# Exponentials of scores and router logits as pieces of their own in the interleaved attention block of a cross-attention and mixture-of-experts kernel

## The chip, the cores and the metric

The kernel runs on one core of a Trainium2 chip. A time is the device time of one execution in microseconds (us). Five engines work side by side, each in the order of its own instruction stream: TensorE (PE in the profile; its weight loads are PEld), VectorE (DVE), ScalarE (ACT), GpSimd (POOL) and SyncE (SP, which here only issues DMAs). They wait for one another through semaphores. An instruction that waits holds up everything behind it on its engine.

## The reference, cut to what matters

The input x has 4 batches of 512 rows of 256 numbers, the context 4 batches of 1024 rows.

```python
x = x + xattn(layernorm(x), ctx, mask)      # 16 heads of 16, 1024 keys, softmax, w_o
h = layernorm(x)                            # from here on the 4 batches attend to each other:
ln1 = layernorm(h)*w1 + b1; q, k, v = split(ln1 @ qkv.T)
p = softmax(q_s,b . k_t,b over earlier positions t)   # axes are (S, B): x's batches are "positions"
h2 = h + attn @ proj.T; ln2 = layernorm(h2)*w2 + b2
gate = softmax(ln2 @ router.T); top 2 of 8 experts
moe = sum over the 2 chosen of gate_e * (gelu(ln2 @ w1[e]) @ w2[e])
x = x + h2 + moe
```

The second block reads its first axis as the sequence, so a row of batch b attends to the same row of batches 0 to b: at most four scores for each head. That is the inner attention block of this case. It needs the rows of batch b after the big cross attention of that batch, and the keys and values of earlier batches.

## The kernel before, in words

**The big attention is the clock of the first stage.** It is cut into 16 groups m (batch m // 4, four heads each), each into 8 steps; a step is called T, from -10 to 128. In a step (loop at the end of the `with ExitStack()` block) PE computes four score tiles of 128x512 for the maxima of the group 10 steps ahead (`maximum`, L1116), which DVE reduces straight from PSUM (L1123, 512 times); four tiles of scores of the group itself (`numerators`, L1137), which ACT turns into exponentials (L1145, 512 times); and four products of the previous step's exponentials with the values (`products`, L1155). From T = 118 on there are no maxima left, so a step is shorter.

**Everything else is woven into these steps by a planner** (class `Plan`). A piece of work has a first and a last step, a cost on PE (`cost`), a cost on DVE (`vector`) and pieces that it must follow by a number of steps (`lag`). `spread` gives each piece a step, by due time, cost per step and a limit on DVE's; `level` then moves pieces to even out the estimated lengths of the steps. Within a step the pieces come after the step's own work, in order of their due times. So when a piece is put into a step, all its instructions on all engines are queued there.

**The inner attention, second layer norm and router of one half of a batch (256 rows) are a generator, `half(b, h)`.** Each `next` runs it to its next `yield`. For b of 0 to 2 the planner's table `PARTS` has one entry for each such part: (PE cost, lag, DVE cost). With their lines, the parts that matter: q, k and v (L438 to L448); the products of queries and keys on POOL (L479); the sums that make scores, their maximum and the subtraction on DVE (L490 to L492), and in the same part their exponential on ACT (L495, 128x64 to 128x128 numbers); normalising (L497 to L499); the products with the values on POOL (L504) and their sum (L515 for the last batch, L522); transposing and projecting (L290, L532, L539); statistics, and the rows written to the output by POOL's addition and an SP DMA (L545 to L548); router logits on PE (L568), their maximum and subtraction on DVE (L579, L580), and in the same part their exponential on ACT (L583); the choice of two experts (L585 to L607); positions in the experts' lists (L615 to L636); four indirect DMAs by POOL that put the rows into a table in DRAM (L659). Batch 0 has no scores to compute, so its generator only yields there.

**Not all of batch 2 is planned into the steps.** `parts[: -1 - 5 * h]` leaves the last part of half (2, 0) and the last six of half (2, 1) to the second stage. Batch 3 (`last`) is done there entirely, and there its exponentials already stand behind a `yield` of their own.

**The second stage** starts when the big attention ends. 39 tiles of 128 rows, each of one expert, are taken from the table (lists a, b, c, d of 9, 8, 9 and 13 tiles, loaded by SP at L800). A tile is transposed (`psxe` L1383, ACT L1386), multiplied by w1 (`psu` L1398), put through gelu on ACT (L1407), transposed (`psg` L1412, ACT L1414), multiplied by w2 (`psy` L1420), scaled on ACT (L1431) and added to the output by an indirect DMA that POOL issues (L1432). Between the tiles' pieces `others` puts the parts of the remaining halves, in an order written down ahead by a small model of the engines' times: the strings at the yields ("D3!" and the like) are its costs.

The generator's parts of batch 2 and the table meet in these lines, which the change touches:

```python
parts = PARTS[:-2] + PADS + PARTS[-2:] if b + h == 0 else PARTS
if b == 2:
    parts = parts[: -1 - 5 * h]
...
last = start + (28, 34, 0)[b] if b < 2 else END - 2 + h
chain = plan.chain(start, last, parts, behind=p, other=chain)
```

`chain` makes part n of the second half wait for part n + 3 of the half before it (`other`).

Of the kernel before, what the change touches and what calls it, by code (L numbers as in the profile page):

```python
# [55 lines left out]
class Plan:  # L56
# [19 lines left out]
    def chain(self, first, last, pieces, behind=None, other=()):  # L76


        slack = last - first - sum(p[1] for p in pieces)
        at = first  # L80
        chain = []
        for n, (cost, lag, vector, f, args) in enumerate(pieces):
            at += lag
            behind = self.add(
                cost,
                at,
                at + max(slack * (n + 1) // len(pieces), 0),
                f,
                *args,
                behind=behind,  # L90
                lag=lag,
                also=other[min(n + 3, len(other) - 1)] if other else None,
                vector=vector,
            )
            chain.append(behind)
        return chain
# [75 lines left out]
def kernel(  # L172
# [226 lines left out]
    def products_of(name, b):  # L399
        if b < B - 1:  # L400
            return k2.tile([P, B - 1, HALF, DK], F32, tag="pr", name=name, bufs=1)
        return late["pool"].tile([P, B, HALF, DK], F32, tag="prlast", name=name, bufs=2)

    def half(b, h):


        n = f"{b}_{h}"
        last = b == B - 1
# [26 lines left out]
        for i in range(2):  # L435
            ps = bank(f"psq{n}_{i}")
            for c in range(KC):
# [4 lines left out]
                    start=(c == 0),  # L442
# [9 lines left out]
        def of_batch(kv, j):  # L452

            return (
                kv[j][:, t0 : t0 + 2, :]
                .rearrange("p t (k d) -> p (t k) d", d=DK)
                .unsqueeze(2)
                .to_broadcast([P, 2 * KVH, REP, DK])
            )

        def grouped(x):
            return x.rearrange("p (k r) d -> p k r d", r=REP)

        if b == 0:

            yield
            yield
            yield
            at = k2.tile([P, HALF, DK], F32, tag="at", name=f"at{n}", bufs=1)
            nc.gpsimd.tensor_copy(grouped(at), of_batch(values, 0))  # L470
            yield
        else:

            def engine(j):
                return nc.vector if last and j % 2 else nc.gpsimd

            pr = products_of(f"pr{n}", b)
            for j in range(b + 1):
                engine(j).tensor_tensor(  # L479
                    grouped(pr[:, j]),  # L480
                    grouped(q.rearrange("p i (h d) -> p (i h) d", d=DK)),
                    of_batch(keys, j),
                    ALU.mult,
                )
            yield "D1.5|G2.4"
            sc = k2.tile([P, B, HALF], F32, tag="sc", name=f"sc{n}")[:, 0 : b + 1, :]
            top = k2.tile([P, HALF], F32, tag="top", name=f"top{n}")
            by_head = sc.rearrange("p j n -> p n j")
            over = [P, b + 1, HALF]
            nc.vector.tensor_reduce(sc, pr[:, 0 : b + 1], AX.X, ALU.add)  # L490
            nc.vector.tensor_reduce(top, by_head, AX.X, ALU.max)
            nc.vector.tensor_tensor(sc, sc, top.unsqueeze(1).to_broadcast(over), ALU.subtract)  # L492
            if last:
                yield "D3!"
            nc.scalar.activation(sc, sc, AF.Exp, scale=SCALE)  # L495
            yield "A2.9"
            nc.vector.tensor_reduce(top, by_head, AX.X, ALU.add)  # L497
            nc.vector.reciprocal(top, top)
            nc.vector.tensor_tensor(sc, sc, top.unsqueeze(1).to_broadcast(over), ALU.mult)  # L499
            yield "D1"  # L500
            at = k2.tile([P, HALF, DK], F32, tag="at", name=f"at{n}", bufs=1)
            pr = products_of(f"pv{n}", b)
            for j in range(b + 1):
                engine(j).tensor_tensor(  # L504
                    grouped(pr[:, j] if j or last else at),
                    of_batch(values, j),
                    sc[:, j, :]
                    .rearrange("p (k r) -> p k r", r=REP)
                    .unsqueeze(3)
                    .to_broadcast([P, 2 * KVH, REP, DK]),  # L510
                    ALU.mult,
                )
            if last:
                yield "D1.5|G2.4"
                nc.vector.tensor_reduce(  # L515
                    at.rearrange("p n d -> p (n d)"),
                    pr.rearrange("p j n d -> p (n d) j"),
                    AX.X,
                    ALU.add,
                )  # L520
            for j in range(1, 1 if last else b + 1):
                (nc.vector if b == 2 else nc.gpsimd).tensor_tensor(at, at, pr[:, j], ALU.add)  # L522
            yield "D2.2!"
# [5 lines left out]
        for i in range(2):  # L529
            ps = bank(f"psp{n}_{i}")  # L530
            for c in range(KC):
# [4 lines left out]
                    start=(c == 0),  # L536
# [29 lines left out]
        for i in range(2):  # L566
            for c in range(KC):
# [4 lines left out]
                    start=(c == 0),  # L572
# [5 lines left out]
        lgs = ps[:, 0 : 2 * E].rearrange("p (i e) -> p i e", e=E)  # L578
        nc.vector.tensor_reduce(m, lgs, AX.X, ALU.max)  # L579
        nc.vector.tensor_tensor(lg, lgs, m.to_broadcast(small), ALU.subtract)  # L580
        if last:
            yield "P1 D0.4!"
        nc.scalar.activation(lg, lg, AF.Exp)  # L583
        yield "A2.8"
        nc.vector.tensor_reduce(m, lg, AX.X, ALU.add)  # L585
# [85 lines left out]
    def pads(chosen, place):  # L671
# [19 lines left out]

    PARTS = [
        (0, 1, 1.7), (0, 2, 1.9), (0.45, 1, 0), (1.3, 1, 0.4), (1.3, 1, 0.4), (0, 1, 0), (0, 2, 1.8),
        (0, 1, 0.8), (0, 1, 0), (0.45, 2, 0), (0.86, 1, 0.5), (0.86, 1, 0.5), (0, 1, 1.4),
        (0, 2, 1.3), (0.45, 1, 0), (0.9, 1, 0.4), (0, 1, 1.7), (0, 1, 1.6), (1.1, 1, 1), (0, 1, 0),
        (0, 1, 0),
    ]
    PADS = [(0, 1, 0), (0, 2, 0), (0, 2, 0), (0, 2, 0)]
# [155 lines left out]
    def project_o(b, t):  # L854
# [10 lines left out]
        nc.vector.tensor_tensor(xt[:, b, t, :], ps[:, 0:D], xt[:, b, t, :], ALU.add)  # L865

    halves = {(b, h): half(b, h) for b in range(B) for h in range(2)}

    with ExitStack() as actx:
# [296 lines left out]
        def compact(dst, src):  # L1166
# [6 lines left out]
        plan = Plan()  # L1173
        START, END = -AHEAD, 8 * M + 1
        chain, queries = (), {}
        divided = [
            plan.add(
# [4 lines left out]
        for b in range(B):  # L1182
            first = 32 * b - 32
            if b:
                turned, projected = [], []
                for kc in range(NKC):
# [8 lines left out]
                        also=turned[kc - KRING] if kc >= KRING else None,  # L1195
# [17 lines left out]
                for h in range(2):  # L1213
# [10 lines left out]
                        also=x,  # L1224
# [10 lines left out]
            for kc in range(NKC):  # L1235
                start = 32 * b - 10 + kc if kc >= 4 else kc if b == 1 else 32 * b - 34 + kc
                start = max(start, START + 1)

                last = min(32 * b + kc - 2, 8 * M - 31)
# [15 lines left out]
            for h in range(2):  # L1255
                start = 32 * b + (40 if b < 2 else 38) + 4 * h
                parts = PARTS[:-2] + PADS + PARTS[-2:] if b + h == 0 else PARTS
                if b == 2:

                    parts = parts[: -1 - 5 * h]  # L1260
                parts = [(cost, lag, vector, next, (halves[b, h], None)) for cost, lag, vector in parts]
                last = start + (28, 34, 0)[b] if b < 2 else END - 2 + h
                chain = plan.chain(start, last, parts, behind=p, other=chain)
                p = None
            if b == 1:
# [74 lines left out]
        for T in range(START, END):  # L1340
            ahead[0] = T < 0
            n, kc = divmod(T, 8)
# [173 lines left out]
    n = 0  # L1516
# [106 lines left out]
```

## Time and profile before

| what | value |
|---|---|
| runs | 872.62, 872.97, 868.33 us; median 872.62 |
| the profiled execution's own time | 868.35 us |
| its span, first to last instruction | 866.6 us |
| first stage, up to the transposes of the last group (L837) | 642.2 us |
| second stage, from there on | 224.4 us |
| PE busy, ACT busy, DVE busy, POOL busy | 816.5, 476.8, 528.7, 311.3 us |
| mean granted PE clock | 0.985 |
| exponentials of the big attention (L1145) | 512, 596 ns each |
| maxima from PSUM (L1123) | 512, 684 ns each |
| exponentials of inner scores (L495), of router logits (L583) | 6 and 8, 282 and 215 ns each |
| additions to the output (L1432) | 39, 3.5 to 5.0 us from issue to landing |

How to read it: busy time is that of an engine's instructions; PE's are pipelined and their ends are modelled, so that PE busy 94% of the span is not PE at its peak. In the views of waits, "A <- B: 8.8, 4, 3.3" says that A sat idle for 8.8 us in total until B, 4 times, at most 3.3 us. In a timeline a row is start, length, engine, line, operation, and in brackets the idle time of the engine before it and what ended it.

### The profile page before, as it was taken

The page shows a single profiled execution, that of the slowest core. Times are in us where ns is not written, and L with a number is a line of the kernel's source. Part 1 is how long each engine was busy: PE and PEld are TensorE (multiplying, and loading weights), DVE is VectorE, ACT ScalarE, POOL GpSimd, SP SyncE. Part 2 cuts the span into 40 slices and gives each one's busy share as a digit, 9 for nine tenths or more (in the row PEclk, how much of TensorE's full clock was granted, in tenths as well). Part 3 has the DMA queues.
Part 4 walks back from the last instruction along what each step waited for, and adds up shares of the span by engine and source line. Part 5 has one row for each costly group of instructions (what it writes and reads, how often), then busy time and mean ns, then how long its engine had stood idle before and what let it go on. Part 6 is the DMA issues. An engine that isn't in the chain of part 4 may idle for free. (4 is left out here: it accounts for less than half of the span.)

```text
span 866.6 us, 14127 instructions
## 1 busy us (share of the span) xinstructions
PE 816.5 (94%) x5031; PEld 390.1 (45%) x5031; DVE 528.7 (61%) x1265; ACT 476.8 (55%) x959; POOL 311.3 (36%) x443
## 2 busy tenths in 40 slices
PE   5999999999999999999999999999989879999980
PEld 4543433334444334443433334333337557667650
DVE  6587666766677677887777778888455586100000
ACT  2326666656665655656656555555665647555430
POOL 7806251002363111579152201233224555433322
PEclk9999999999999999999999999999899999999996
DMA  7249003334000000001000009200212222552222
GB/s 228 57 133 301 17 1 118 110 99 128 2 1 1 25 14 13 34 17 51 1 1 1 13 2 334 99 20 2 69 38 55 53 36 58 121 98 27 29 31 24
DMA packets 46597, 53.30 MB, mean 62 GB/s; under 512 B 4782, under 2 KB 40580, under 8 KB 46528
## 3 DMA queue, kind: packets, MB, share of 16 engines
q1 hardware_dynamic: 37952, 41.42, 15.8%
q0 software_dynamic: 7920, 10.50, 6.9%
q8 instruction: 41, 0.67, 0.3%
q10 hardware_dynamic: 656, 0.48, 0.2%
q14 instruction: 28, 0.23, 0.1%
HBM read 22.43 MB, written 31.09 MB: 62 GB/s over the span
## 5 line engine op out<-in xcount | busy, mean ns | idle before, releaser
L1123 DVE TENSOR_REDUCE mx<-psm 128x1 f32<-128x512 f32 x512 | 326.6, 684 | 131.0 <-PE pss L1137 117.5
L1145 ACT ACTIVATE ex<-pss 128x512 f32<-128x512 f32 x512 | 277.5, 596 | 208.4 <-PE pss L1137 201.3
L1116 PE MATMUL psm<-kT_odd,shared 32*128 32x512 f32 x512 | 153.1, 639 | 1.1 <-DVE mx L1123 0.9
L1137 PE MATMUL pss<-qt,shared 32*128 32x512 f32 x512 | 152.7, 640 | 0.0
L1137 PE MATMUL pss<-qt,kT_odd 32*128 32x512 f32 x512 | 146.7, 649 | 0.5 <-ACT ex L1145 0.5
L1116 PE MATMUL psm<-shared 32*128 32x512 f32 x512 | 144.5, 639 | 2.2 <-ACT shared L1104 2.2
L1155 PE MATMUL av<-ex,vaug 128*32 128x512 f32 (+1 forms) x880 | 107.7, 559 | 0.0
L962 POOL TENSOR_TENSOR shared<-shared 128x256 f32<-128x256 f32 x44 | 33.3, 758 | 133.8 <-ACT shared L1005 101.7
L1420 PE MATMUL psy<-shared 128*128 x312 | 75.3, 383 | 4.6 <-ACT shared L1414 4.3
L1398 PE MATMUL psu<-shared 128*128 x156 | 76.0, 606 | 1.0 <-ACT shared L1431 0.4
L1116 PEld LDWEIGHTS psm<-kT_odd,shared 32*128 32x128 f32 x512 | 43.9, 183 | 72.5 <-DVE mx L1123 29.6
L1116 PEld LDWEIGHTS psm<-shared 32*128 32x128 f32 x512 | 43.3, 183 | 67.9 <-DVE mx L1123 25.7
L1420 PEld LDWEIGHTS psy<-shared 128*128 128x128 f32 x312 | 56.1, 190 | 13.4 <-ACT shared L1414 7.6
L1155 PEld LDWEIGHTS av<-ex,vaug 128*32 128x32 f32 x880 | 17.7, 108 | 84.3 <-issue 80.8
L659 POOL DMA_INDIRECT table<-rows,index x32 | 31.8, 994 | 53.8 <-issue 29.0
L264 POOL TENSOR_TENSOR rm<-vm,power 128x2 f32<-128x2 f32 x8 | 5.7, 712 | 117.6 <-DVE vm L545 114.7
L1137 PEld LDWEIGHTS pss<-qt,kT_odd 32*128 32x128 f32 x512 | 42.8, 186 | 8.3 <-issue 5.3
L1137 PEld LDWEIGHTS pss<-qt,shared 32*128 32x128 f32 x512 | 44.3, 183 | 0.6 <-ACT ex L1145 0.6
L964 POOL TENSOR_TENSOR shared<-shared 128x128 f32<-128x128 f32 x88 | 44.5, 527 | 0.0
L1407 ACT ACTIVATE shared<-psu 128x512 f32<-128x512 f32 x39 | 23.5, 603 | 26.1 <-PE psu L1398 26.0
L1398 PEld LDWEIGHTS psu<-shared 128*128 128x128 f32 x156 | 26.6, 192 | 19.6 <-issue 13.3
L1432 POOL DMA_INDIRECT out_dram<-shared,numberd x13 | 20.1, 1544 | 39.5 <-ACT shared L1431 29.9
(299 smaller groups left out, 1124.8 us busy)
## 6 DMA issues: line engine op xcount, KB each, us to landing
table<-zeros SPq DMA_DIRECT2D x8, 2120.0 KB, 17.6
shared<-in_moe_w_dram SPq DMA_DIRECT2D x16, 512.0 KB, 10.1
shared<-in_ctxT_dram SPq DMA_DIRECT2D x8, 512.0 KB, 4.1
shared<-table SPq DMA_DIRECT2D x18, 132.5 KB, 2.1
xt<-in_x_dram SPq DMA_DIRECT2D x4, 512.0 KB, 8.1
out_dram<-xt SPq DMA_DIRECT2D x8, 256.0 KB, 2.2
rows_d<-table SPq DMA_DIRECT2D x13, 132.5 KB, 2.4
rows_b<-table SPq DMA_DIRECT2D x8, 132.5 KB, 2.2
```

The lines of the kernel that those rows point to most:

```text
L659: inst = nc.gpsimd.indirect_dma_start(out=table, out_offset=bass.IndirectOffsetOnAxis(ap=index, axis=0), in_=rows, in_offset=None, bounds_ ...
L962: engine.tensor_tensor(a, src, over(f[:, 0:DK]), ALU.mult)
L964: engine.tensor_tensor(r[:, :, i::2], src[:, :, 1 - i :: 2], over(f[:, DK + i : 2 * DK : 2]), ALU.mult,)
L1116: nc.tensor.matmul(ps, q1[m][rows, t * P : (t + 1) * P], kT[b % 2][rows, g, h * 512 : (h + 1) * 512], start=True, stop=True,)
L1123: nc.vector.tensor_reduce(mx[m][:, t, j, h : h + 1], ps, AX.X, ALU.max)
L1137: nc.tensor.matmul(ps, kT[b % 2][rows, g, kc * P : (kc + 1) * P], q2[m][rows, :], start=True, stop=True,)
L1145: nc.scalar.activation(ex[m, kc, j], ps, AF.Exp, scale=SCALE)
L1155: nc.tensor.matmul(av[m][32 * j : 32 * j + 32, over], vaug[(b * NKC + kc) % VRING][:, 4 * g + j, :], x[:, over], start=(kc == 0), stop=(kc ...
L1398: nc.tensor.matmul(ps_of[k], xT_of[k][:, c, :], w1_sb[:, bass.ds(weights_of[k] + c * F, F)], start=(c == 0), stop=(c == KC - 1),)
L1407: nc.scalar.activation(h_of[k], ps_of[k], AF.Gelu_apprx_tanh)
L1420: nc.tensor.matmul(ps_of[k], h_of[k][:, f * P : (f + 1) * P], w2_sb[:, bass.ds(weights_of[k] + f * D, D)], start=(f == 0), stop=(f == F // ...
L1432: nc.gpsimd.indirect_dma_start(out=out.rearrange("b s d -> (b s) d"), out_offset=bass.IndirectOffsetOnAxis(ap=number[name][:, i, :], axis= ...
```

## The change: what it does

It makes the exponential of the scores and that of the router logits parts of their own for every batch, so that the planner puts each at least one step behind the DVE part that prepares it. The table gets two entries more, each without PE or DVE cost; the generator of batch 0, which has no scores, yields once more; in `chain` the wait for the half before goes from part n + 3 to n + 4; and batch 2 is cut at another place. Both halves of batch 2 still have 20 and 15 parts in the first stage, but since two (one) of them are the new ones, half (2, 0) now stops three parts before its end (its positions, L615 to L636, and both pairs of its table DMAs go to the second stage) and half (2, 1) stops before its transposes for the router (L290). Both are due at END - 1.

```diff
@@ Plan.chain
-                also=other[min(n + 3, len(other) - 1)] if other else None,
+                also=other[min(n + 4, len(other) - 1)] if other else None,
@@ half
         if b == 0:
-            yield
-            yield
-            yield
+            for _ in range(4):
+                yield
...
             nc.vector.tensor_tensor(sc, sc, top.unsqueeze(1).to_broadcast(over), ALU.subtract)
-            if last:
-                yield "D3!"
+            yield "D3!"
             nc.scalar.activation(sc, sc, AF.Exp, scale=SCALE)
             yield "A2.9"
...
         nc.vector.tensor_tensor(lg, lgs, m.to_broadcast(small), ALU.subtract)
-        if last:
-            yield "P1 D0.4!"
+        yield "P1 D0.4!"
         nc.scalar.activation(lg, lg, AF.Exp)
         yield "A2.8"
...
     PARTS = [
         (0, 1, 1.7), (0, 2, 1.9), (0.45, 1, 0), (1.3, 1, 0.4), (1.3, 1, 0.4), (0, 1, 0), (0, 2, 1.8),
-        (0, 1, 0.8), (0, 1, 0), (0.45, 2, 0), (0.86, 1, 0.5), (0.86, 1, 0.5), (0, 1, 1.4),
-        (0, 2, 1.3), (0.45, 1, 0), (0.9, 1, 0.4), (0, 1, 1.7), (0, 1, 1.6), (1.1, 1, 1), (0, 1, 0),
+        (0, 1, 0), (0, 1, 0.8), (0, 1, 0), (0.45, 2, 0), (0.86, 1, 0.5), (0.86, 1, 0.5), (0, 1, 1.4),
+        (0, 2, 1.3), (0.45, 1, 0), (0.9, 1, 0.4), (0, 1, 0), (0, 1, 1.7), (0, 1, 1.6), (1.1, 1, 1), (0, 1, 0),
         (0, 1, 0),
     ]
@@ the planning of the halves
                 if b == 2:
-                    parts = parts[: -1 - 5 * h]
+                    parts = parts[: -3 - 5 * h]
                 parts = [(cost, lag, vector, next, (halves[b, h], None)) for cost, lag, vector in parts]
-                last = start + (28, 34, 0)[b] if b < 2 else END - 2 + h
+                last = start + (28, 34, 0)[b] if b < 2 else END - 1
                 chain = plan.chain(start, last, parts, behind=p, other=chain)
```

## The prediction

> **What bounds the kernel now.** I read the page's busy shares and its chain first, then the busy times by stage, then the waits and timelines of the steps that are longer than others of their cost, then the second stage's output chain.
>
> ```profile
> PE 816.5 (94%) x5031; PEld 390.1 (45%) x5031; DVE 528.7 (61%) x1265; ACT 476.8 (55%) x959; POOL 311.3 (36%) x443
> ```
> ```profile
> 237.00:600.00 363.00, 359.45 (x2460) 145.85 (x2456) 281.23 (x664) 212.83 (x421) 126.72 (x178) 1.00 0.11 37
> 600.00:642.20 42.20, 41.46 (x254) 15.13 (x250) 23.57 (x83) 27.70 (x56) 9.73 (x11) 0.92 0.17 49
> 642.20:733.20 91.00, 80.21 (x370) 55.90 (x371) 55.88 (x177) 52.73 (x108) 44.33 (x39) 0.98 0.24 48
> 733.20:866.60 133.40, 109.76 (x472) 74.48 (x469) 7.62 (x37) 58.84 (x129) 47.29 (x32) 0.94 0.34 56
> ```
>
> Columns of the second: stretch and length; busy us of PE, PEld, DVE, ACT, POOL; granted PE clock. Up to 642 us PE sets the pace; DVE and ACT have room on average, so only a *late* instruction of theirs costs time. I took the length of each step from the start of its first exponential (L1145) to the next step's: lengths repeat to 0.05 us by planned PE cost (0.45: 4.06; 0.86: 4.20; 1.31: 4.59; 1.72: 5.06). Steps 40 to 116 take 366.7 us where these medians give 353.3. Four of the long ones hold an inner score part:
>
> ```profile
> ACT sc L495 <- DVE sc L492: 8.8, 4, 3.3
> ```
>
> Step 83 is the plainest:
>
> ```profile
> 448.07 1.21 DVE L490 TENSOR_REDUCE sc<-pr 128x64 f32<-128x1024 f32 x1
> ...
> 449.57 0.23 DVE L492 TENSOR_TENSOR sc<-sc,top 128x64 f32<-128x64 f32 x1
> 449.71 1.28 DVE L1123 TENSOR_REDUCE mx<-psm 128x1 f32<-128x512 f32 x2
> 449.83 0.26 ACT L495 ACTIVATE sc<-sc 128x64 f32<-128x64 f32 x1 [1.78 <-DVE sc L492]
> 449.99 0.57 ACT L1104 COPY shared<-psqt 128x512 f32<-128x512 f32 x1
> ...
> 450.61 0.69 PE L1116 MATMUL psm<-shared 32*128 32x512 f32 x1 [0.25 <-ACT shared L1104]
> ```
>
> ACT stands 1.78 us at the small exponential; behind it wait two copies out of PSUM and the next step's exponentials; PE waits for a copy. In step 117 it is worse:
>
> ```profile
> 608.89 0.28 ACT L495 ACTIVATE sc<-sc 128x96 f32<-128x96 f32 x1 [3.33 <-DVE sc L492]
> ```
> ```profile
> 612.00:619.00 7.00, 7.00 (x31) 1.37 (x32) 2.69 (x7) 3.58 (x8) 5.01 (x5) 0.53 0.20 59
> ```
>
> After 3.33 us of it PE gets score banks only as fast as ACT empties them (eight matmuls in 3.7 us), and then the clock halves for 6.8 us.
>
> The second stage ends on a chain of output additions, each waiting for the one before: 3.8 us of DMA and 0.7 around it. It becomes unbroken here:
>
> ```profile
> 716.91 1.25 POOL L547 TENSOR_TENSOR xt<-xt,h 128x512 f32<-128x512 f32 x1
> 718.50 0.46 ACT L1431 ACTIVATE shared<-psy,gateb 128x256 f32<-128x256 f32 x1
> 721.15 1.60 POOL L1432 DMA_INDIRECT out_dram<-shared,numberb  x1 [2.99 <-ACT xT L297]
> ```
>
> The tenth addition's input is ready at 718.96, but half (3,1)'s rows go to the output first: POOL adds until 718.16, SP issues at 718.19, landing takes 2.2 us. The timeline names another releaser, but this one fits. From 721.15 to the last addition at 858.63 there are 29 intervals of 4.74 us.
>
> **The change part by part.** Sums are made against the profiled execution: 868.35 us, span 866.6. The runs' median is 872.62, 4.3 above; two of three runs lie there.
>
> *Score exponentials of batch 1* (steps 83, 88). They exceed their medians by 1.29 and 1.60; the following steps get 0.23 and 0.24 back. Net 2.4. With the exponential a step later its input is long ready: ACT pays 0.26 us where it has two in a step of four free. What is late next: DVE, since the sums (1.66 us, three instructions) still stand before the next maxima. A step of 4.2 to 5.1 us less 2.5 for maxima leaves 1.7 or more, so I let nothing remain. Gain 2.4, bounds 1 to 2.9.
>
> *Those of batch 2.* Steps 111 to 113 take 14.41 for 12.62. In the changed plan the sums of half (2,0) (2.3 us) and the normalising of half (2,1) (2.9) both fall on step 112: 5.2 us of DVE against 1.4 free. So DVE's lateness takes the place of ACT's wait, and I count 0 (-1.5 to +1.8). Step 117's sums now fall on 118, which has no maxima. From 601.81 to the second stage's start (642.21) takes 40.4 us; at undisturbed lengths (4.2, then 2.1 + 1.1 x cost, planned cost 6.83, 1.8 at the end) it is 34.5. I take back the wait of 3.33, and 0.7 because the planned cost drops to 6.14. Gain 4.0; 1 if DVE is late here too, 7 if the clock stays up.
>
> Here the Trainium skill speaks against part of that: "TensorE: Matmul & The Clock Gate", Part 1, has the clock halve after an idle window of about 3.4 us. In the trace no wait of PE before 612 exceeds 1.1 us, yet it halved after the starved stretch. By the page the dip isn't the wait's doing and stays (4.0 at most); by the row it goes with it (up to 7). I take 4.0, short of the row.
>
> *Router exponentials.* Six waits, 2.5 us in all, 0.4 each; steps with them are mostly at their medians (60: 5.09 for 5.06). I count 0, bounds 0 to 1.
>
> *The replanned rest.* Some 50 pieces move. In step 53 a transposed query (L1104) is made just before its first use: 6.32 for 4.62. The new plan makes it in step 50: gain 1.7. Planned costs of steps 40 to 116 give 0.9 less. Against this DVE work piles up at steps 100 to 102 (3.5, 2.0, 3.0 planned) and 106: by the excess of steps 47 and 107 (1.3, 0.7), a loss of 1.0, bounds 0 to 4.
>
> First stage: 2.4 + 0 + 4.0 + 1.7 + 0.9 - 1.0 = 8.0.
>
> *Work moved to the second stage.* PE gets four transposes (0.44) and five small matmuls (1.05), which leave the first stage. Half (2,1)'s router exponential now comes after the first gelu, so ACT changes its function table once more each way. In the trace a change is the load alone (717.09, 1.28 us; exponential at 718.38): 2.6 for both. The skill's "ScalarE: Activation LUTs", section "What ACT_TABLE_LOAD costs", adds about 1.38 of drain: 5.3. By the row it hides: between the second and the third tile's psu PE has 4.1 us of other work in the changed order (psp, psy, psg and psxe rows). By the page about 1.2 would show. I take the row: 0.
>
> POOL's queue changes more. The four table DMAs of half (2,1) (1.3 us each, 656.8 to 661.6) stood right before the first addition, which went at 662.89 with its input ready at 658.0. Now half (2,0)'s four come first and half (2,1)'s lie in pairs between the first additions, each covered by the 4.5 us in which POOL waits for a landing. SP's row loads of list b wait for them: now later, but they were done at 675 and first used at 700.
>
> *Batch 3 in POOL's order.* The products of half (3,0) (679.5, 37.3 us into the stage) stood behind the fourth addition, held by the third's landing; now behind the third. DVE's last sum of half (3,1) no longer stands behind g8b (3.1) and the statistics of half (3,0). But both output writes of batch 3 now stand one tile earlier: after them 30 intervals remain for 29, +4.7. Following the changed order by hand with the durations above, half (3,1)'s write lets the ninth addition go 71.7 us into the stage, where the tenth went at 78.9: 7.3 earlier. Net gain 2.6; bounds -4 (no earlier) to +7 (what PE idles up to there, 12, less what must stay).
>
> Sum: 868.35 - 8.0 - 2.6 = 857.7 on the profiled execution's scale, 862.0 at the median.
>
> **The rivals.**
> *DVE was the limit anyway* (0.16): with the wait gone, DVE's sums delay maxima by as much; seen already in steps 111 to 113. First stage gains 3, the second nothing: 869.6. Against: step 83, where ACT alone holds the copy.
> *The second stage gives it back* (0.18), slower. Place: PE in tile 8, where the transposes of half (3,1)'s attention now come about 1.5 tiles earlier in PE's order, and the ninth addition behind its write. If batch 3's chain isn't earlier in time, PE waits there and the chain is one interval longer: +4.7, table changes at the page's price +2.7, the lost clock as now; the first stage gains 2. 872.6 + 5.4 = 878. It decides once the ninth addition goes later than 77 us into the stage. For it: every wait in between (at <- POOL, gelu <- POOL) is tight. Against: POOL's order, and DVE's.
> *More of it* (0.13): the clock stays up and batch 3's chain loses its waits: 11 + 7 off: 854.6.
> *It doesn't do what it says*: excluded by the order of the changed program, where each exponential follows the next step's.
>
> **How the numbers follow.** Forecast 0.53. Half a per cent, 4.4 us, is about what a measurement here can tell from no change. Faster than 868.3: forecast and "more", less a little for a small gain, 0.64; within: 0.18; slower: 0.18. The range takes in "more" and the DVE rival and stops before the second stage's rival: 853 to 876.
>
> **What would show it.** Right: ACT's waits at L495 in the first stage under 1 us in all; steps 84 and 89 near their medians; the second stage (L837) starting at about 634; no halved clock near 612; the ninth addition about 72 us into the stage, then 4.7 us steps. Wrong: long steps at 101 to 103 and 113 with DVE behind; PE waiting for L515 in tile 8; the stage from L837 to the end longer than 224.4 us.

## The result: slower by 1.5%, and the profile after

The changed kernel takes 883.51 us (median of 6 runs, 878.57 to 885.83) where the kernel before, now with 6 runs, takes 869.3 (868.33 to 872.97): ratio 1.0146, 95% interval 1.0113 to 1.0179. Predicted were 862.0, with 853 to 876 as the range. Its profiled execution took 882.34 us, span 880.6, for 868.35 and 866.6.

Line numbers of the changed kernel are two or three below those of before: maxima L1120, exponentials L1142, psd L834, score exponential L493, output additions L1429. Tiles in PSUM are called by what they hold: psm scores for a maximum, pss scores of the group itself, psp a projection, psa and psx transposed attention and transposed rows, psd the transposes of a group's results. Each takes a bank, and PE can write the next tile into that bank only when the reader of the one before is through. First the busy row, then the stages, cut where those of before were cut (2.3 us into step 116, at about the first psd of the last group, and 91 us after that):

```profile
PE 823.1 (93%) x5031; PEld 393.3 (45%) x5031; DVE 535.9 (61%) x1265; ACT 480.2 (55%) x961; POOL 311.5 (35%) x443
```
```profile
238.00:607.30 369.30, 362.30 (x2448) 144.52 (x2444) 281.74 (x657) 213.54 (x421) 123.90 (x176) 0.99 0.11 37
607.30:655.00 47.70, 40.54 (x256) 15.18 (x253) 27.87 (x85) 26.84 (x54) 9.84 (x11) 0.89 0.14 37
655.00:746.00 91.00, 81.91 (x382) 58.51 (x380) 61.81 (x199) 56.37 (x112) 48.88 (x42) 0.96 0.26 54
746.00:880.60 134.60, 111.72 (x472) 75.76 (x470) 4.36 (x21) 58.76 (x129) 45.56 (x31) 0.93 0.33 53
```

The number of DVE's instructions is the same, 1265, yet they take 7.2 us more: some got slower. The stretch up to step 116 is 6.3 us longer, the next 5.5, and PE's clock is lower in all four. The second stage (first psd at 654.59 for 642.21) takes 226.0 us for 224.4. So 12.4 of the 14.0 us by which the span grew are lost in the first stage, 1.0 of them before its first exponential.

What the change set out to do, it did. The source view of the score exponential in the first stage:

```profile
L493 ACT ACTIVATE sc<-sc x4: 258/274/305, 457.7 to 624.7; 128x64 f32<-128x64 f32 x2, 128x96 f32<-128x96 f32 x2
```

No idle time is listed behind it, where the kernel before had 8.8 us in four waits. Steps that were long before are short now, and others are long (us from a step's first exponential to the next step's):

| step | 47 | 53 | 83 | 88 | 112 | 119 | 66 | 72 | 101 | 113 | 116 | 123 |
|---|---|---|---|---|---|---|---|---|---|---|---|---|
| before | 5.92 | 6.32 | 5.88 | 5.80 | 6.55 | 5.62 | 4.94 | 4.59 | 4.20 | 4.37 | 4.09 | 4.02 |
| after | 5.06 | 4.16 | 4.75 | 4.16 | 3.47 | 3.13 | 6.38 | 8.47 | 7.77 | 6.30 | 8.91 | 8.25 |

Two of the long ones, read closely. DVE's timeline around step 72, which starts at 392.2:

```profile
388.71 1.29 DVE L1120 TENSOR_REDUCE mx<-psm 128x1 f32<-128x512 f32 x2 [0.78 <-PE pss L1134]
389.91 0.70 DVE L600 SCALAR_TENSOR_TENSOR left<-picks,lg 128x16 f32<-128x16 f32 x1
...
392.23 0.67 DVE L604 TENSOR_TENSOR rows<-lg,chosen 128x16 f32<-128x16 f32 x1
392.82 0.41 DVE L862 TENSOR_TENSOR xt<-psp,xt 128x256 f32<-128x256 f32 x1
393.16 0.68 DVE L1120 TENSOR_REDUCE mx<-psm 128x1 f32<-128x512 f32 x1
394.45 0.69 DVE L1120 TENSOR_REDUCE mx<-psm 128x1 f32<-128x512 f32 x1 [0.61 <-PE pss L1134]
397.89 1.29 DVE L1120 TENSOR_REDUCE mx<-psm 128x1 f32<-128x512 f32 x2 [2.75 <-PE pss L1134]
```

Part 20 of half (0, 1), the choice of the second expert, stands on DVE ahead of the addition that reads project_o(1, 3) from PSUM (L862). Maxima and such pieces take banks from one ring, so PE can't write the next maxima's scores until that bank is read, at 393.2: it waits 1.2 us. Then its clock halves, from 394.8 to 398.2. And step 116, all engines:

```profile
604.59 1.48 DVE L520 TENSOR_TENSOR at<-at,pv 128x512 f32<-128x512 f32 x2
...
606.22 3.83 POOL L478 TENSOR_TENSOR pr<-q,keys 128x512 f32<-128x512 f32 x3 [2.04 <-DVE lna L720]
...
606.83 0.80 DVE L732 TENSOR_TENSOR lna<-lna,done 128x8 f32<-128x8 f32 x1
607.66 1.24 DVE L701 TENSOR_TENSOR pairsa<-earlier,lna 128x64 f32<-128x64 f32 x1
608.94 0.22 DVE L706 TENSOR_REDUCE excla<-pairsa 128x8 f32<-128x64 f32 x1
609.20 0.87 DVE L707 TENSOR_TENSOR incla<-excla,lna 128x8 f32<-128x8 f32 x1
609.99 2.47 DVE L1120 TENSOR_REDUCE mx<-psm 128x1 f32<-128x512 f32 x4
...
610.73 1.12 PE L834 MATMUL psd<-ident,oraw 128*128 128x128 f32 x4 [3.38 <-DVE mx L1120]
```

DVE makes the additions of half (2, 0) and the first part of list a before it comes to the step's maxima. Three of the list's instructions take 0.80, 1.24 and 0.87 us here, while POOL multiplies. In the kernel before, they were 0.17, 0.22 and 0.17 long:

```profile
598.43 0.17 DVE L735 TENSOR_TENSOR lna<-lna,done 128x8 f32<-128x8 f32 x1
598.63 0.22 DVE L704 TENSOR_TENSOR pairsa<-earlier,lna 128x64 f32<-128x64 f32 x1
598.89 0.22 DVE L709 TENSOR_REDUCE excla<-pairsa 128x8 f32<-128x64 f32 x1
599.14 0.17 DVE L710 TENSOR_TENSOR incla<-excla,lna 128x8 f32<-128x8 f32 x1
```

The maxima are late by additions and list, PE stands 3.38 us, and its clock halves for 6.8 us.

### The profile page after: what moved, and what is told of

Read it like the earlier page. It is cut to its first block, busy times and chain, and to the rows that moved or that the text cites. A ratio compares the mean times of both kernels' runs of the same rounds, so it can differ in the third digit from the quotient of the medians.

```text
span 880.6 us, 14128 instructions
## 1 busy us (share of the span) xinstructions
PE 823.1 (93%) x5031; PEld 393.3 (45%) x5031; DVE 535.9 (61%) x1265; ACT 480.2 (55%) x961; POOL 311.5 (35%) x443
## 4 chain that ended last, share of the span: by engine, by line
PE 76%; DVE 8%; DMA 8%; issue 2%; ACT 2%; POOL 2%; POOLq 0%; ACTq 0%; DVEq 0%
PE psm L1113 29%; PE av L1152 14%; DMA out_dram<-shared,numberd 5%; PE psu L1395 4%; PE psy L1417 4%; PE psv L1027 3%; PE psk L994 3%; PE psq L438 3%; DMA out_dram<-shared,numberc 2%; PE pss L1134 2%; DVE mx L1120 2%; PE psqt L1093 2%; PE pskt L1015 2%; PE psp L855 1%; PE psp L530 1%
## 5 line engine op out<-in xcount | busy, mean ns | idle before, releaser
L1120 DVE TENSOR_REDUCE mx<-psm 128x1 f32<-128x512 f32 x512 | 327.3, 685 | 142.3 <-PE pss L1134 127.4
L1142 ACT ACTIVATE ex<-pss 128x512 f32<-128x512 f32 x512 | 278.0, 596 | 220.5 <-PE pss L1134 213.0
L1113 PE MATMUL psm<-kT_odd,shared 32*128 32x512 f32 x512 | 155.1, 654 | 1.3 <-DVE xt L862 1.3
L1113 PE MATMUL psm<-shared 32*128 32x512 f32 x512 | 147.1, 649 | 1.9 <-DVE xt L862 1.2
L1417 PE MATMUL psy<-shared 128*128 x312 | 78.3, 393 | 5.2 <-ACT shared L1411 5.1
L961 POOL TENSOR_TENSOR shared<-shared 128x128 f32<-128x128 f32 x88 | 44.6, 528 | 0.0
L1027 PE MATMUL psv<-shared 128*128 128x256 f32 x128 | 34.8, 394 | 0.5 <-DVE mx L1120 0.5
```

Of the source, the lines that this page charges most:

```text
L961: engine.tensor_tensor(r[:, :, i::2], src[:, :, 1 - i :: 2], over(f[:, DK + i : 2 * DK : 2]), ALU.mult,)
L1027: nc.tensor.matmul(ps[:, 0:D], context(b, kc, c), wv_sb[:, c, :], start=(c == 0), stop=(c == KC - 1),)
L1113: nc.tensor.matmul(ps, q1[m][rows, t * P : (t + 1) * P], kT[b % 2][rows, g, h * 512 : (h + 1) * 512], start=True, stop=True,)
L1120: nc.vector.tensor_reduce(mx[m][:, t, j, h : h + 1], ps, AX.X, ALU.max)
L1142: nc.scalar.activation(ex[m, kc, j], ps, AF.Exp, scale=SCALE)
L1417: nc.tensor.matmul(ps_of[k], h_of[k][:, f * P : (f + 1) * P], w2_sb[:, bass.ds(weights_of[k] + f * D, D)], start=(f == 0), stop=(f == F // ...
```

## The experiments

**Theories.** *Plan*: the exponentials' own step is harmless, and the loss comes from where the replanned pieces meet on DVE and POOL, ahead of maxima or of banks that PE waits for. *Split*: a small exponential in a part of its own is itself what costs. The kernel before is measured again beside each group of runs: 868.3 us beside e1 to e4, 869.79 beside e5 to e8, 867.28 beside e9 to e12, 869.75 beside e13 and e14. Ratios are against it; since it differs by up to 2.5 us, runs of different groups are compared by their ratios. Step lengths come from one profile for each kernel. Line numbers differ by a few from kernel to kernel.

**1. e1: the old plan, only the four score exponentials a step later.**

```diff
@@ kernel before, half
-            if last:
-                yield "D3!"
+            yield "D3!"
@@ behind plan.spread
+        for T, bh in ((86, (1, 0)), (89, (1, 1)), (115, (2, 0)), (120, (2, 1))):
+            steps[T][0:0] = [(next, (halves[bh], None))]
```

> The plan of before, with only the four score exponentials of batches 1 and 2 issued one step later (steps 84, 89, 113, 118); every other instruction stays in its step, but for two products of POOL and their normalising, which follow by a step. Theory 'plan' (the split itself gains what the prediction said, and the loss of the changed kernel comes from the pieces that the planner moved): steps 83, 88 and 117 lose their waits, 2.4 + 4, so 863 to 867 us beside 869 to 873 before, steps 72, 101 and 123 as before. Rival 'split' (a small exponential in a part of its own is itself what delays DVE and the maxima behind it): slower than before by 5 or more, with long steps at 84, 89, 113, 118.

869.61 us, ratio 1.0017 (1.0007 to 1.0028): neither theory. By step the gains are there: 83 took 4.59, 88 4.59, and 112 and 113 together 9.70 for 10.92. Then 116 took 7.70 and 121 5.99. One `next` more at 115 had moved the products and additions of half (2, 0) from 114 to 115, beside list a's work, the same neighbours as in the changed kernel. The list's instructions took 0.80, 1.25 and 0.87 us here too.

**2. e5: the same, with those products left where they were** (the added `next` in steps 84, 89, 113, 118).

> The plan of before with the four score exponentials a step later, but now the normalising stays in its step (84, 113, 118, just behind the exponential) and the products of POOL stay too (114, 119), where the first such run had moved the products of half (2,0) to 115, beside the list work. In that run the wait at 117 had gone, yet steps 116 (7.70 for 4.09) and 121 (5.99 for 2.64) grew. Theory 'neighbours on DVE' (a step grows when DVE's queue before the maxima grows, whatever was moved there; POOL's products beside it slow small DVE instructions from 0.2 to 0.8 and 1.25 us): 116 and 121 go back to 4.1 and 2.6, 112, 83, 88, 117 stay short: 861 to 865 us beside 868.3. Rival (the split's wait is only passed on from ACT to DVE): 867 to 870, with 116 or 118 long again.

867.91 us, ratio 0.9983 (0.9972 to 0.9994): faster than e1, but above the 861 to 865 expected. The list work, in the same step as in the run before:

```profile
595.41 0.17 DVE L734 TENSOR_TENSOR lna<-lna,done 128x8 f32<-128x8 f32 x1
595.61 0.22 DVE L703 TENSOR_TENSOR pairsa<-earlier,lna 128x64 f32<-128x64 f32 x1
595.87 0.22 DVE L708 TENSOR_REDUCE excla<-pairsa 128x8 f32<-128x64 f32 x1
596.12 0.17 DVE L709 TENSOR_TENSOR incla<-excla,lna 128x8 f32<-128x8 f32 x1
```

Step 116 is back at 4.10, and step 121 begins 8.1 us earlier than in the kernel before, 2.9 of which may be chance: e13 below, with the wait at 117 still in it, spends that much less on steps 119 and 120, where its clock isn't halved. But then step 121 takes 8.28:

```profile
610.25 0.72 POOL L264 TENSOR_TENSOR rm<-vm,power 128x2 f32<-128x2 f32 x1 [15.54 <-DVE vm L544]
610.96 1.26 POOL L546 TENSOR_TENSOR xt<-xt,h 128x512 f32<-128x512 f32 x1
...
612.18 1.04 POOL L503 TENSOR_TENSOR at<-values,sc 128x512 f32<-128x512 f32 x1
...
613.20 2.05 POOL L503 TENSOR_TENSOR pv<-values,sc 128x512 f32<-128x512 f32 x2
...
614.27 2.33 DVE L521 TENSOR_TENSOR at<-at,pv 128x512 f32<-128x512 f32 x2 [4.10 <-POOL pv L503]
...
616.65 1.12 PE L290 MATMUL psa<-ident,at 128*128 128x128 f32 x4 [3.79 <-DVE at L521]
```

From DVE's statistics, past POOL's 5.1 us and DVE's additions, to PE's transposes it is a chain of some 6.4 us. Without maxima a step is 2.1 to 2.4 us, and the plan gives the chain two steps. The transposes stand in PE's order ahead of the next scores, so PE waits 3.8 us and its clock halves for 6.8. The step-117 wait, once removed, came back as this one.

**3. e9: the later parts of half (2, 1) one step later.**

```diff
@@ e5, the list of added parts
-(118, (2, 1))
+(118, (2, 1)), (125, (2, 1)), (128, (2, 1))
@@ behind it
+        for T in (121, 126):
+            steps[T].remove((next, (halves[2, 1], None)))
```

> As the run with the score exponentials late and POOL's products kept, and half (2,1)'s later parts one step later each: its transposes (psa) from 121 to 122, its projections at 123 and 124, statistics at 125, transposes of rows at 128. In that run everything was 8.1 us early at step 121, then PE stood 3.8 us at psa, behind the additions that DVE starts only when POOL is through (POOL is busy for 5.1 us: 0.7, 1.3, 3.1), and the clock halved after it. Theory 'the tail is a chain through DVE, POOL, DVE, PE that the shorter steps do not give time': step 121 goes from 8.28 to about 2.6 and 122 by less than 1.5 longer, so 3 to 5 us: 863 to 866. Rival (the second stage begins no earlier, since its input hangs on that same chain): 867 to 869.

865.23 us, ratio 0.9974 (0.9961 to 0.9987). The number lies in the theory's range, but only because the kernel before was 2.5 us faster beside this group: by ratio e9 is 0.8 us below e5, where 3 to 5 were expected, and the intervals overlap. Step 121 is 2.42, as expected; 122 is 6.68 for 4.97 and keeps part of it: now the transposes of half (2, 0)'s rows wait behind the same additions.

```profile
617.56 0.87 PE L290 MATMUL psx<-ident,rows 128*128 128x128 f32 x4 [2.65 <-DVE rows L555]
```

**4. e11 and e14: one piece more, and those rows later.** e11 has `transpose_q(8)` in step 50 for 53; e14 also moves half (2, 0)'s parts from 122 to 127 on by a step.

> As the run with half (2,1)'s parts later, and one more piece from the changed plan: the transposed query 8 in step 50 and not in 53, just before its first use. The prediction put 1.7 us on it (step 53 6.32, 4.62 being usual). Theory: 1.7 to 2 below that run, so 861 to 864. Rival (the copy of the query delays ACT in step 50 as much): no difference.

> As the run with the query early and half (2,1) later (865.0), and the parts of half (2,0) from the transposes of its rows on one step later (123 to 128 for 122 to 127). There PE stood 2.65 us in step 122 for those rows, whose normalising stands on DVE behind the additions that wait for POOL. Theory 'the same chain': step 122 goes from 6.9 to under 4.5 and the end of the first stage comes 1.5 to 3 us earlier: 862.5 to 864. Rival (the stall moves to step 123 or to the start of the second stage, which needs these parts): 865 to 867.

e11: 864.98 us, 0.9968 (0.9952 to 0.9984), no resolved difference from e9. In the trace step 53 loses 1.77 and step 50 grows by 0.43, so both theories hold in part. e14: 865.87 us, 0.9954 (0.9941 to 0.9967) beside its own 869.75. Step 122 is 5.18 for 6.87 (under 4.5 was expected); counted from the first exponential, the second stage starts 6.5 us earlier than in the kernel before, in e11 4.4. It is the fastest version by ratio, though the intervals of e9, e11 and e13 overlap. Not all that the first stage gains is kept: in the profiles of e5, e9, e11 and e14 the second stage is 226.1 to 227.3 us long, for 224.4 before. In e5, e11 and e14 the last 28 intervals between output additions are 1.4 to 3.1 us longer in all; what sets these, and where the rest comes from, was not tried.

**5. e2 and e12: the router exponentials late as well.** e2 adds five parts to e1, in steps 74, 70, 98, 106, 128, for the five routers of the first stage; e12 adds them to e5 in steps 61, 67, 98, 104, 124, so that no other part moves.

> As the run with the four score exponentials late, and the five router exponentials of the first stage a step later too (steps 61, 67, 98, 104, 124), plan of before. Theory 'plan': within 2 us of the run with scores alone, since router exponentials waited 0.4 us each: 863 to 867. Rival 'split': slower than before, by more than with scores alone, 878 to 885.

> As the run with score exponentials late and products kept (867.9 beside 869.8), and the five router exponentials at the head of the next step's pieces, all other parts where they were in the kernel before (in the first run of routers some had moved on: the table writes of half (0,0) from 72 to 74, where step 74 took 9.1). Theory 'the router exponentials are worth nothing by themselves, the moved parts were the cost': within 1.5 us of 867.9. Rival (the routers' split costs by itself): 873 or more.

e2: 878.02 us, ratio 1.0118 (1.0092 to 1.0144), the number of the rival, but not its place. Steps 74 and 75 took 9.12 and 7.08: the last table writes of half (0, 0) had moved there, and half (0, 1) was a step later. Waits in these two steps:

```profile
...
DVE mx L1122 <- PE psm L1115: 3.6, 1, 3.6
ACT shared L1004 <- POOL shared L963: 3.3, 1, 3.3
PEld psm L1115 <- ACT shared L1004: 3.1, 1, 3.1
PE psm L1115 <- ACT shared L1004: 2.2, 1, 2.2
```

POOL issued DMAs of 1 us each, its rotation of keys (L961 to L969) was late, ACT stood at a copy that needs it, and PE at the bank. e12: 869.34 us, ratio 1.0027 (1.0018 to 1.0036). Steps 61, 67, 98 and 104 kept their lengths to 0.02 us; step 126 took 5.56 for 3.41, DVE waiting 2.8 us for the exponential of half (2, 0) because its normalising stayed in the same step. So the split of a router exponential gains nothing, and in the last one, where steps are short, it costs 2.1 us. By ratio e12 is 3.8 us above e5, so the theory (within 1.5) did not hold; where the rest comes from was not tried.

**6. e3: the changed kernel with its exponentials early again.** Its plan is kept and the new part left empty.

```diff
@@ changed kernel, half; likewise for the router
-            yield "D3!"
+            if last:
+                yield "D3!"
             nc.scalar.activation(sc, sc, AF.Exp, scale=SCALE)
+            if not last:
+                yield "D3!"
```

> The changed kernel with its plan untouched, but with each exponential of the first stage issued in the part of its DVE work again (the part of its own stays, empty), so that ACT waits for it as in the kernel before. Theory 'plan': the loss stays and the waits come back: 884 to 890 us, steps 72, 101, 116, 123 long as in the changed kernel, and step 83 at 5.9. Rival 'split': the loss goes, 868 to 874.

884.49 us, ratio 1.0191 (1.0173 to 1.0208). Steps 101, 116 and 123 are as long as in the changed kernel (8.02, 8.91, 9.88), 72 is 6.91, 83 is back at 6.20. The loss is there without the split: *split* has fallen.

**7. e4: the attention parts as replanned, the 55 other pieces as before.**

> The changed kernel, with the attention parts and list parts in their new steps, but the other 55 pieces (divisions, projections, transposes, statistics) given the steps that they have in the kernel before. Theory 'plan, other pieces': project_o(1,3) stays in step 71 but division 13 goes back to 114 and division 14 to 125; the stalls at 116 and 123 vanish, 116 by 4.9 and 123 by 5.1, and so most of 14: 868 to 873 us. Rival within the plan theory, 'parts of the halves themselves' (what they queue on DVE in steps 71, 100, 112, 121): stalls at 72 and 101 stay, 876 to 884. Rival 'split': 880 to 884.

884.52 us, ratio 1.0186 (1.0163 to 1.0209): a miss. Step 72 is mended (4.59), 123 partly (5.88), but 61 (7.77), 64 (6.96) and 75 (7.84) are long instead, and 101 and 116 stay (8.22, 7.86). So the moves of attention and list parts are enough to lose as much, with other steps long; the moves of the 55 other pieces alone were not tried.

**8. e6, e7, e8, e10: taking the meetings of the changed kernel apart.** e6 issues pieces with DVE work alone last within a step; e7 puts list a's three parts (in 115, 117 and 119 in the changed plan) into 117, 118 and 119, and division 14 into 125 (121); e8 does both; e10 also has the products of half (2, 1) in step 120.

```diff
@@ e6: Plan.spread, the order inside a step
+        alone = lambda n: self.pieces[n][7] > 0 and not self.pieces[n][0]
-        for n in sorted(range(len(self.pieces)), key=lambda n: (self.pieces[n][2], n)):
+        for n in sorted(range(len(self.pieces)), key=lambda n: (alone(n), self.pieces[n][2], n)):
@@ e7: steps set by hand behind level (320 to 322 list a, 14 the division)
+GIVEN = {117: (320,), 118: (321,), 119: (322,), 125: (14,)}
```

> The changed kernel and its plan; inside each step the pieces with VectorE work alone (statistics, sums, routing, list work) are issued last, so that a PSUM bank that DVE reads (project_o, divide, psp) is read ahead of them. Theory 'a bank held behind DVE's queue': step 72 (8.47) and step 101 (7.77), where project_o(1,3) and project_o(2,1) stand behind routing work, go back to 4.6 and 4.2; 113, 116 and 123 have the cause in other steps and stay: 874 to 878 us beside 883.5. Rival (DVE has too much in these steps, in any order): within 2 us of 883.5.

> The changed kernel with five pieces moved: the list work of list a from steps 115, 117, 119 to 117, 118, 119 (117 has the last maxima) and division 14 from 121 back to 125. Theory: step 116 (8.91, maxima behind the slowed list work and the wait for POOL's products) and step 123 (8.25, the division's bank behind the same wait) lose 3 to 4 each, and the clock stays up there, 2 to 3 more: 874 to 878 us. Rival (the wait for POOL's products at the additions alone holds the maxima of 116): only 123 is mended, 879 to 881.

> Both edits of the two runs before in one kernel. If the two causes are independent, the sum of their gains: 865 to 871 us, no slower than the kernel before. If a stall only moves on to the next step, clearly less: 874 or more.

> The changed kernel with both edits of before (banks first, list work and division 14 late), and POOL's products and additions of half (2,1) from step 121 to 120. There step 123 is still 8.0, PE standing 2.7 us at psa behind the same chain and the clock halved. Theory: with 2.4 us more for the chain step 123 loses 3 to 4: 868 to 870 us. Rival (the products start no earlier, since POOL's power and addition of half (2,0) stand before them and wait for DVE): within 1 us of the 872.6 of that run.

| run | us | ratio (interval) | step 72 | 101 | 116 | 123 |
|---|---|---|---|---|---|---|
| changed kernel | 883.51 | 1.0146 (1.0113 to 1.0179) | 8.47 | 7.77 | 8.91 | 8.25 |
| e6 | 878.81 | 1.0100 (1.0074 to 1.0127) | 4.59 | 6.11 | 8.92 | 8.20 |
| e7 | 875.80 | 1.0071 (1.0054 to 1.0088) | 10.11 | 6.57 | 4.06 | 6.56 |
| e8 | 872.58 | 1.0030 (1.0015 to 1.0045) | 4.59 | 6.11 | 4.06 | 8.04 |
| e10 | 868.65 | 1.0018 (1.0005 to 1.0030) | 4.59 | 6.11 | 4.06 | 8.17 |

DVE in step 72 of e6, the same instructions in another order:

```profile
390.59 0.41 DVE L863 TENSOR_TENSOR xt<-psp,xt 128x256 f32<-128x256 f32 x1
390.92 0.36 DVE L601 SCALAR_TENSOR_TENSOR left<-picks,lg 128x16 f32<-128x16 f32 x1
...
393.39 1.27 DVE L1121 TENSOR_REDUCE mx<-psm 128x1 f32<-128x512 f32 x2
394.88 1.29 DVE L1121 TENSOR_REDUCE mx<-psm 128x1 f32<-128x512 f32 x2 [0.22 <-PE pss L1135]
```

The bank is read at once, and the four maxima are through 2.8 us after the first began, not 6.0: in step 72 the order in DVE's queue was the whole cause (4.59 is its length before), in 101 less than half. 878.81 is just above the 874 to 878 expected. e7 mends 116 entirely: its list instructions are back at 0.17 to 0.23 us and stand behind the last maxima. At 123 it gains 1.7 us of the 3 to 4 expected; PE now waits for psa there, the chain of e5. The two edits nearly add up (0.46 and 0.75 in 100, together 1.16), though 872.58 stays above the 865 to 871 expected. In e8's profile the second stage starts at 642.96 us, against 654.59 in the changed kernel and 642.21 before: 11.6 of the 12.4 us lost in the first stage are back, by the order within steps and the place of a few pieces alone. e10's number lies in its range, but again beside a faster kernel before: by ratio it is 1.0 us below e8, with overlapping intervals, as its rival had it. Step 123 is unchanged, only that PE now stands 3.2 us for psx there, where in e8 it stood 2.7 for psa. In its profile step 113 is 1.1 us shorter, and the second stage, from psd on, 4.6, of which 3.8 lie in the last 28 output intervals (4.66 us each for 4.79). Why, these runs don't show.

e7 and the changed kernel issue the same instructions up to step 114, yet step 72 takes 10.11 in one and 8.47 in the other. PE waits 1.2 us in both; the clock is halved for 6.8 us from 393.2 in e7, for 3.4 from 394.8 in the changed kernel. 3.4 us more of the halved clock cost 1.64. At steps 101 and 113 it is the other way round: the clock stays up in e7 and is halved for 3.4 us in the changed kernel, which takes 1.31 more over steps 101 and 102 and 1.48 more over 113 and 114. So e7's 6.57 at step 101 isn't its edit's doing, and beside it the order of e6 (6.11, also at full clock) is worth 0.5 there at most, not 1.7.

**9. e13: the second stage's share alone.** The kernel before, with the three last planned parts of batch 2 left to the second stage.

```diff
@@ kernel before, behind plan.spread
+        for T, bh in ((126, (2, 0)), (127, (2, 0)), (127, (2, 1))):
+            steps[T].remove((next, (halves[bh], None)))
```

> The kernel before, with the last two parts of half (2,0) and the last part of half (2,1) left to the second stage, as many as the changed plan leaves there; nothing else moves, and no exponential is split. Theory of the prediction: the first stage 0 to 1 us shorter, the second 2.6 shorter with the ninth addition 71.7 us into it: 865 to 867 us beside 869. Rival 'PE stands at the transposes of half (3,1)'s attention in tile 8, and the chain has one addition more': ninth addition at 75, second stage 225.5 to 227, 869 to 872 us.

866.99 us, ratio 0.9968 (0.9946 to 0.9990). The ninth addition is 72.4 us into the stage, as the prediction's working had it (71.7), but the stage takes 224.3 us for 224.4: the 30 intervals from there are 4.79 us long, for 4.74. The first stage is 2.5 us shorter, counted from its first exponential. The edit accounts for 1.35 of it: step 126 takes 2.07 for 3.42. Another 1.0 has nothing to do with the edit: with the same order of instructions up to step 125 the clock isn't halved after step 117 (it was, for 6.8 us, in the kernel before), so that steps 119 and 120 take 5.84 for 8.70; but step 121 gives 2.0 of that back (4.66 for 2.64), with PE waiting 1.6 us for psa.

## Why the prediction was wrong, step by step

The sum missed the profiled execution by 24.6 us (857.7 against 882.34): 15.1 in steps 40 to 116, where a gain of 4.0 was forecast and 11.1 were lost; 4.3 from step 117 to the second stage; 4.2 in the second stage; 1.0 before the first exponential. Term by term:

- *Score exponentials of batch 1, 2.4.* Right. Alone (e5) they gave 1.07 at steps 83 and 84 and 0.98 at 88 and 89: 2.05. In the changed kernel 0.7 are left, since other pieces stand in these steps.
- *Those of batch 2 in steps 111 to 113, 0.* Right in sum: 112 to 114 take 15.78 us for 15.98. That it comes out so near is in part luck: e7, with the same instructions and the clock up, takes 14.30.
- *Step 117, 4.0.* The wait went, and e5 is 5.1 us faster over steps 117 to 120 (2.2 faster than e13, which has the wait but not the halved clock); then the chain through DVE, POOL, DVE and PE gives it back at 121. In the changed kernel the way from step 117 to the second stage takes 40.7 us for 40.4. What I missed is what is late next: POOL's products and DVE's additions for psa, two steps ahead of it.
- *Router exponentials, 0.* Right for four of five (e12); the fifth costs 2.1 us.
- *Step 53, 1.7.* The step lost 2.16. By itself (e11) the moved query gave 1.77 there and took back 0.43 in step 50.
- *Planned costs, 0.9.* Under 1 by the medians too, and of no account against the next point.
- *"Against this DVE work piles up at steps 100 to 102 (3.5, 2.0, 3.0 planned) and 106 [...] a loss of 1.0, bounds 0 to 4."* **This is the step that failed.** Steps 40 to 116 exceeded their medians by about 13 us before and by about 25 after. The excesses over 1 us that went (47, 53, 83, 88, 112) make 8.4; those that came (66, 72, 82, 101, 113, 114, 116) make 18.4, and 123, behind these, has another 4.2 over its length before. I sized the term by the planned DVE sums, and the plan has 2.0 at step 71, 2.2 at 115 and 0 at 123: nothing to see there. The sums do not hold what made these steps long: the order on DVE's queue, a bank behind other work (e6: 3.9 at step 72, of which some 1.6 are the clock's by the price above; 0.5 at most at 101); additions that the table counts as 0, but that take 1.5 to 2.3 us and wait for POOL; small DVE instructions that grow about fivefold beside POOL (at step 116 it is the meeting of the two that costs: 3.6 us less with the additions elsewhere, e1 and e5, and 4.9 less with the list work elsewhere, e7); and the clock, which halves at five of these stalls (steps 72, 101, 113, 116, 123).
- *Second stage, 2.6 shorter.* It is 1.6 longer, 4.1 above the forecast: 3.3 us since the ninth addition goes 75.0 us in and not 71.7, 0.6 since the 30 intervals from there are 4.76 us, 0.2 at its end. The moved parts alone do not do that (e13: 72.4, though no gain either). In the changed kernel PE stood for psa in tile 8, one of the signs I had put under "wrong":

```profile
PE psa L290 <- DVE at L513: 4.5, 2, 3.7
```

In e13 this is 3.6 with 2.2 at the longest, in the kernel before 4.2 and 2.6. Besides, the clock was halved at 705.4 and at 725.9, each time for 3.4 us (in e13 once, at 699.9). How much of the 3.3 us is the clock's was not separated.

Of the rivals *"DVE was the limit anyway"* had the kind of cause, but took it to be only the moved sums, and so ended at 869.6. The slower one, in the second stage, had the smaller of the two places. The range stopped at 876, short of that rival; e4 shows another mixture of the same moves at much the same price, 16 us.

On the clock, the skill's rule (an idle window of about 3.4 us) was set against a row where it had halved without such a wait. The row was read a little too short: PE had also waited 1.26 us once, in step 53, with no halving behind it. But the runs side with it: the clock halves at step 72 after a longest wait of 1.2 us. The same page, "TensorE: Matmul & The Clock Gate", has both things elsewhere: in "What's actually happening" the window runs freely, 3.41 us long, and all halved stretches here are 3.4 us or multiples of it, but for the one that runs into the end of the kernel; and "A second HAM failure mode: psum-queue depth-cycling" tells of a clock that drops on frequent short idling between groups of matmuls.

The trace shows more than the longest wait does. All changes of the clock in it lie on one grid of 3.41 us. In the changed kernel's windows of that grid from 300 us to the end of the first stage, PE is busy for 2.23, 2.15, 1.65, 0.88 and 1.38 us in the five right before the clock halves (from 391.4, 531.4, 589.4, 606.5 and 633.8), and for 2.49 or more in all others at full clock. So there it is the idle time of a window in sum that goes with the halving, and how a stall falls on the grid can differ between executions of one order. No sharp limit comes out of this: in e13 a window with 1.74 us (from 618.0) is not followed by it, and before the halving in the kernel before PE counts as busy throughout (3.41 from 608.4, with eight slow matmuls in it).

In the first stage, from its first exponential on, the clock is halved for 20.5 us in the changed kernel (394.8, 534.8, 592.8, 609.9, 637.2) and for 6.8 before. At 1.3 to 1.6 us for each 3.4, as measured against e7, that is 5.2 to 6.6 of the 11.4 us lost from there on, as an estimate; the rest is waiting itself.

## What to carry to other kernels

Where small work is woven into the steps of a pipeline, the cost of moving a piece doesn't show in its own row alone: read, in the changed order, what each engine has in its queue ahead of the instruction that releases PE's next bank, and price that, with work on other engines that it waits for. Taking out a wait is worth its length only up to the next link; give that link the time too (e5 to e14: 0.17 to 0.46 in 100 faster), and don't let a planner move fifty other pieces in the same edit. If they are moved, put the instructions that free a PSUM bank first.

## What the runs showed of the hardware

- DVE instructions with two SBUF inputs grow while POOL multiplies: from 0.17 to 0.80, from 0.22 to 1.24 and from 0.17 to 0.87 us; the reduction between them, with one input, stays at 0.22. "GPSIMD Engine Reference" of the skill, section "1. Specifications", says just that: SBUF interfaces shared with VectorE, contention with instructions that have two SBUF inputs. I had not looked for it in the plan.
- One and the same order of instructions can have the clock halved for 6.8 us or not at all (before and e13, steps 119 and 120). That is 2.9 us in these two steps, but only 1.0, or 0.1% of the kernel, once the next wait for psa has taken its part; seen in one profile each.
- The interval between output additions varies from profile to profile: the last 28 take 4.65 us each in the changed kernel, 4.74 in the kernel before and 4.85 in e5, up to 5.5 us of the whole. The second stages of two single profiles can differ by that much for this reason alone; whether the kernel or chance sets it was not separated.
